# Moving one image's convolutions out of the head and running the last image's final stage in three lanes

## The chip, the cores and the metric

The kernel runs on one core of a Trainium2 chip. The metric is the device time of one execution in microseconds; the median of the runs is taken. A core has five engines that run their own instruction queues in order and wait for one another on semaphores: TensorE (PE, matmuls into PSUM), VectorE (DVE), ScalarE (ACT, activation functions from a loaded table set), GpSimd (POOL) and SyncE (SP), whose queue issues the kernel's DMAs.

## What is computed

Four layers follow one another on x of shape (4, 64, 64, 128), four images of 4096 pixels with 128 channels. The change touches layers 0 and 1 and the point at which layer 2 begins. Both are state-space scans in four directions over the pixels of an image:

```python
# layer 0, per image
left, right = jnp.split(x, 2, axis=-1)
right = _silu(_bn(_conv1x1(right, cv1_w), cv1_g, cv1_b))
xr = _ss2d(right, ...)            # in_proj, depthwise 3x3, Silu, four scans, norm, * silu(z), out_proj
l = _silu(_bn(_conv1x1(left, cv2_w), cv2_g, cv2_b))
l = _bn(l, bn0_g, bn0_b)
l = jax.nn.relu(_bn(_conv3x3(l, c1_w, c1_b), bn1_g, bn1_b))
l = jax.nn.relu(_bn(_conv3x3(l, c2_w, c2_b), bn2_g, bn2_b))
l = jax.nn.relu(_conv1x1(l, c3_w) + c3_b)
xr = _silu(_bn(_conv1x1(xr, cv_w), cv_g, cv_b))
out = _silu(_bn(_conv1x1(jnp.concatenate([l, xr], -1), cv3_w), cv3_g, cv3_b))   # shuffled, + x

# the scan of both layers, per direction
h = jnp.exp(d_t[..., None] * A) * h + (d_t * x_t)[..., None] * B_t[:, :, None, :]
y_t = jnp.einsum('bkdn,bkn->bkd', h, C_t)

# the end of layer 1, per image
y = _ln(y, onorm_w, onorm_b) * _silu(z)
x = input + y @ out_proj_w
h2 = _ln(x, ln2_w, ln2_b)
h2 = jax.nn.gelu(h2 @ fc1_w + fc1_b, approximate=False) @ fc2_w + fc2_b
return x + h2
```

Note that the 3x3 convolutions of layer 0 work on the left half of the channels. The scan of layer 0 doesn't read their result; it is joined to the scan's result afterwards.

## The kernel before

Everything is held channel by pixel: 128 partitions, an image's 4096 pixels along the free axis, worked on in eight chunks of 512 pixels (NCH = 8, T = 512) or, in the scans, in four steps of 1024 (TS).

The scans (class Scans, L240) are 3072 units: 12 tasks (one for each image in layer 0, two for each image in layer 1) of 4 directions, 4 steps and 16 groups. For each unit PE spreads the step sizes (L406), ACT takes the exponential in PSUM (L408), POOL forms the product dbu from a DMA'd tile dub and repB (L398), DVE scans (L418), copies a state (L428) and multiplies with repC (L430), and PE sums (L453). `run` issues this in a fixed order, u units ahead for each stage, and `prepare` makes the next step's operands.

Beside the scans runs the side work (class Side, L532): `pre0` (L786, before a layer 0 scan), `post0` (L844, after it), `pre1` (L888) and `post1` (L922) around the scans of layer 1. They are generators that yield the engine their next step needs. `order` (L988) lists them with the scan after which and before which each is due; PIECES (L984) gives the number of steps of each. After each unit `between` (L1034) hands out a credit of at least PACE = 0.83 steps, issues steps that `Lane.fits` lets through, and issues without asking when a due unit has come (`late`). Times in the planner (class Plan, L115) are estimates written by hand; it decides only the order in which instructions are issued. Stores of the side work are posted and issued later, on SP's queue.

Two pieces of side work stand outside the scans. `pre0(0)`, the head, runs before the first scan: per chunk a projection cv1 and cv2, Silu, the two halves of in_proj and a Silu of z; then `depthwise` (L676), eight half-image passes with a Silu each; then twice `conv` (L713), the 3x3 convolutions, and c3. Only after that does the first task fetch xc (L283) and prepare its first step. `post1(3)`, the tail, runs after the last scan, one chunk after the other: load y and silu(z), a norm over 256 channels (`norm`, L750), product, output projection, add, a norm over 128 channels, fc1 in four parts, Gelu, fc2, add, store. All side tiles and the side's PSUM bank `ms` have one buffer (`fetch` and `pad` two).

Every Silu and Gelu of the side work goes through `act` (L633), which puts the table set of Ln and Exp, the one the scans need, back at once:

```python
def act(self, out, in_, func, **kw):
    self.nc.scalar.activation(out, in_, func, **kw)
    self.nc.scalar.preload_act_table_set("natural_log_exp_and_others")
```

Side instructions go through a counting wrapper, so they all carry line L98 in the profile and are told apart by their tiles. After the tail the pools of the scans are given back and layer 2 (class Edges, L1073) takes the memory: it loads its weights (L1091 to L1097), folds constants, clears near and vals (L1171, L1174) and starts with statistics of image 0 (L1191 to L1210).

Of the kernel before, what the change touches and what calls it, by code (L numbers as in the profile page):

```python
# [9 lines left out]
F32 = mybir.dt.float32  # L10
# [7 lines left out]
P = 128  # L18
H = 64
HW = 64  # L20
L = HW * HW
T = 512
NCH = L // T
# [4 lines left out]
TS = 1024  # L28
# [86 lines left out]
class Plan:  # L115
# [16 lines left out]
    def start(self):  # L132
        self.at = dict(PE=0.0, ACT=0.0, POOL=0.0)
        self.done, self.running = 0.0, True
# [105 lines left out]
class Scans:  # L240
# [27 lines left out]
    def tile(self, name, bufs, tag=None, shape=(P, TS), dtype=F32):  # L268
        return self.pool.tile(list(shape), dtype, name=name, tag=tag or name, bufs=bufs)

    def bank(self):
        return self.psum.tile([P, T], F32, name="mp", tag="mp", bufs=1)
# [259 lines left out]
class Side:  # L532
# [100 lines left out]
    def act(self, out, in_, func, **kw):  # L633

        self.nc.scalar.activation(out, in_, func, **kw)
        self.nc.scalar.preload_act_table_set("natural_log_exp_and_others")

    def fetch(self, name, src):
        t = self.tile(name, bufs=2)
# [145 lines left out]

    def pre0(self, b):  # L786

        nc = self.nc
        wt = self.weights(self.d0a)
        cv12, inp, c3 = wt[:, 0:P], wt[0:H, P : 3 * P], wt[:, 3 * P : 3 * P + H]  # L790
        cw = wt[:, 3 * P + H :].rearrange("p (n t c) -> p n t c", n=2, t=6)
        lo, hi = slice(0, H), slice(H, P)
        x = self.fetch("x", self.x0[b, :, chunk(0)])
        for c in range(NCH):
            yield ("PE", self.landed) if c == 0 else "PE"
            ps = self.bank()
            nc.tensor.matmul(ps, cv12, x, start=True, stop=True)
            if c + 1 < NCH:
                x = self.fetch("x", self.x0[b, :, chunk(c + 1)])
            yield self.when("TAB", "d0")  # L800

            rl = self.tile("d0")
            self.act(rl, ps, AF.Silu, scale=self.cv12g, bias=self.cv12b)
            yield "PE POOL"
            l = self.tile("sq")
            nc.gpsimd.tensor_scalar(l[hi], rl[hi], self.bn0g[hi], self.bn0b[hi], ALU.mult, ALU.add)
            ps = self.bank()
            nc.tensor.matmul(ps, inp[:, 0:P], rl[lo], start=True, stop=True)
            yield self.when("ACT", "d1")
            xi = self.tile("d1")  # L810
            nc.scalar.copy(xi, ps)
            self.store("d1", self.xid[0, b, 0][:, chunk(c)], xi)
            self.store("sq", self.ld[b][0][:, chunk(c)], l[hi])
            yield "PE"
            ps = self.bank()
            nc.tensor.matmul(ps, inp[:, P : 2 * P], rl[lo], start=True, stop=True)
            yield self.when("TAB", "o")
            sz = self.tile("o")
            self.act(sz, ps, AF.Silu)
            self.store("o", self.szd[0, b, 0][:, chunk(c)], sz)  # L820
        yield from self.depthwise(self.dww0, self.dwb0, self.xid[0, b, 0], self.xcd[0, b, 0])
        for i in range(2):
            for item in self.conv(cw[:, i], self.ld[b][i]):
                if isinstance(item, str) or isinstance(item[0], str):
                    yield item
                    continue
                c, ps = item
                l = self.tile("d0")
                nc.scalar.activation(l, ps, AF.Relu, scale=self.bn12g[i], bias=self.cb[:, i : i + 1])
                if i == 0:  # L830
                    self.store("d0", self.across(self.ld[b][1], 0, H, c), l)
                    yield "PE"
                    continue
                yield "PE"
                ps = self.bank()
                for half in (lo, hi):
                    nc.tensor.matmul(ps[half, :], c3[half], l[half], start=True, stop=True)
                yield self.when("ACT", "o")
                o = self.tile("o")
                nc.scalar.activation(o, ps, AF.Relu, bias=self.c3b)  # L840
                self.store("o", self.across(self.catd[b], 0, H, c), o)
                yield "PE"
# [76 lines left out]
        for ct in range(2):  # L919
            yield from self.depthwise(self.dww1[:, ct, :], self.dwb1[:, ct, :], self.xid[1, b, ct], self.xcd[1, b, ct])  # L920

    def post1(self, b):  # L922
        nc = self.nc
        wt = self.weights(self.w1b)
        outp, fc1 = wt[:, 0:256].rearrange("p (t c) -> p t c", t=2), wt[:, 256:768]
        fc2 = wt[:, 768:1280].rearrange("p (t c) -> p t c", t=4)

        def start(c):
            big = self.tile("big", shape=(P, 4, T))
            for ct in range(2):  # L930
                nc.sync.dma_start(out=big[:, ct, :], in_=self.yd[1, b, ct][:, chunk(c)])
            for ct in range(2):
                nc.sync.dma_start(out=big[:, 2 + ct, :], in_=self.szd[1, b, ct][:, chunk(c)])
            self.landed = nc.now + FOUR_LANDING
            return [big[:, i, :] for i in range(2)], [big[:, i, :] for i in range(2, 4)]

        ys, szs = start(0)
        yield "PE", self.landed
        for c in range(NCH):
            ns = []  # L940
            yield from self.norm(ys, ns, "ACT")
            x = self.fetch("x", self.x1[b, :, chunk(c)])
            for ct, n in enumerate(ns):
                nc.scalar.activation(n, n, AF.Identity, scale=self.onw[:, ct : ct + 1], bias=self.onb[:, ct : ct + 1])
                yield "POOL"
                nc.gpsimd.tensor_mul(n, n, szs[ct])
                yield "ACT" if ct == 0 else "PE"
            ps = self.bank()
            for ct, n in enumerate(ns):
                nc.tensor.matmul(ps, outp[:, ct, :], n, start=ct == 0, stop=ct == 1)  # L950
            yield "ACT"
            x2 = self.tile("x2")
            nc.scalar.copy(x2, ps)
            yield "POOL"
            nc.gpsimd.tensor_add(x2, x2, x)
            yield "PE"
            ns = []
            yield from self.norm([x2], ns, "PE")
            (h2,) = ns
            hid = self.tile("hid", "big", (P, 4, T))  # L960
            for m in range(4):
                ps = self.bank()
                nc.tensor.matmul(ps, fc1[:, m * P : (m + 1) * P], h2, start=True, stop=True)
                yield "ACT"
                nc.scalar.activation(hid[:, m, :], ps, AF.Identity, bias=self.bias1[:, 4 + m : 5 + m])
                yield "PE" if m < 3 else "TAB"
            self.act(hid, hid, AF.Gelu)
            yield "PE"
            ps = self.bank()
            for m in range(4):  # L970
                nc.tensor.matmul(ps, fc2[:, m, :], hid[:, m, :], start=m == 0, stop=m == 3)
                yield "PE" if m < 3 else "ACT"
            o = self.tile("o")
            nc.scalar.activation(o, ps, AF.Identity, bias=self.fc2b)
            yield "POOL"
            nc.gpsimd.tensor_add(o, o, x2)
            if c + 1 < NCH:
                ys, szs = start(c + 1)
            yield "PE", self.landed
            self.store("o", self.x2[b, :, chunk(c)], o)  # L980

PIECES = dict(pre0=156, post0=114, pre1=172, post1=290)  # L984
PACE = 0.83


def order(nb):  # L988

    scans = [(layer, b) for layer in range(2) for b in range(nb)]
    side = []
    for b in range(1, nb):
        side.append(("pre0", b, None, (0, b)))
    side.insert(2, ("post0", 0, (0, 0), None))
    side.append(("pre1", 0, (0, 0), (1, 0)))
    for b in range(1, nb):
        side += [("post0", b, (0, b), None), ("pre1", b, (0, b), (1, b))]
    side += [("post1", b, (1, b), None) for b in range(nb - 1)]  # L1000
    at = {which: n for n, which in enumerate(scans)}
    side = [(name, b, at.get(after, -1), at.get(before, len(scans))) for name, b, after, before in side]
    return scans, side


def scan_layers(tc, C, nb, x_in, d0, s0, d1, s1, out):

    nc = tc.nc
    with ExitStack() as es:
        pool = es.enter_context(tc.tile_pool(name="scan", bufs=1))  # L1010
        side_pool = es.enter_context(tc.tile_pool(name="side", bufs=1))
        psum = es.enter_context(tc.tile_pool(name="psum", bufs=1, space=PSUM))
# [43 lines left out]
                credit -= 1.0  # L1056

        with tc.manual_schedule():
            for _ in side.pre0(0):
                pass  # L1060
            scans.run(between)
            plan.flush("side")
            plan.running = False
            for _ in side.post1(nb - 1):
                pass


NB = 9
# [766 lines left out]
```

## Time and profile before

| what | value |
|---|---|
| median of 3 runs | 14693.77 us (14692.58 to 14696.81) |
| the profiled execution | 14702.13 us, its span 14700.3 us |
| mean granted PE clock | 0.711 |
| first scan (L418) starts | 319.99 us |
| last scan starts | 11716.3 us |
| 3072 scans of DVE (L418), mean | 2.35 us with a state, 2.29 us without |
| hc products of DVE (L430), mean | 1.22 us |
| ACT_TABLE_LOAD of the side work, x640 | 821.1 us, 1.28 us each |
| first matmul of the tail | 11736.29 us |
| last add of the tail ends | 12154.6 us |

The profile is one execution. A row of the timeline gives start, duration, engine, line, operation, out<-in tiles, sizes and, in brackets, the idle time of the engine before it and what ended that. A row of the stages gives busy time and instruction count of each engine in that stretch, the share of full speed that the PE clock was granted, and the DMA engines' busy share and rate. L98 stands for all side work.

### The profile page before, as it was taken

Reading aid. Unit: us, or ns where it says so; the run is one execution under the profiler, and the core shown is the slowest. Engines: PE = TensorE matmul, PEld = TensorE weight load, DVE = VectorE, ACT = ScalarE, POOL = GpSimd, SP = SyncE. Lnnn points to the kernel's source line nnn. Section 1 sums busy time; section 2 is a strip of 40 time slices with the busy share of each in tenths; the row PEclk is TensorE's granted clock in tenths of the full one; section 3 lists DMA queues with packets and bytes.
Section 4 is the critical chain, followed back from the end, with each engine's and each line's share of the span. In section 5 each row is a group of like instructions: output and inputs, shape, how many; then the busy total and the mean of one; then the engine's idle time right before and its main releaser. Section 6 shows DMA issues by size and latency. Waiting matters only on the chain. (4 is left out here: it accounts for less than half of the span.)

```text
span 14700.3 us, 125581 instructions
## 1 busy us (share of the span) xinstructions
PE 10730.8 (73%) x36776; PEld 2755.0 (19%) x36776; DVE 12416.1 (84%) x10627; ACT 7877.7 (54%) x9279; POOL 9851.6 (67%) x4742
## 2 busy tenths in 40 slices
PE   5777777777776677777767767777776657777999
PEld 1111111111111111111111111111111112223555
DVE  1999999999999999999999999999999904565666
ACT  3645466555656565566555555555555335543555
POOL 1877788777888788788778888888888713441000
PEclk7676676766667666667667776667766568777999
DMA  4888888888888988988888777787787600002000
GB/s 113 220 207 218 204 216 222 216 214 217 216 224 215 224 208 208 230 217 211 216 213 213 199 195 200 197 208 200 196 205 193 166 30 24 20 18 48 13 14 8
DMA packets 853732, 2490.00 MB, mean 169 GB/s; under 512 B 143031, under 2 KB 164287, under 8 KB 844855
## 3 DMA queue, kind: packets, MB, share of 16 engines
q1 hardware_dynamic: 853047, 2481.97, 67.1%
q8 instruction: 295, 4.83, 0.1%
q14 instruction: 390, 3.19, 0.1%
HBM read 2060.21 MB, written 270.27 MB: 159 GB/s over the span
## 5 line engine op out<-in xcount | busy, mean ns | idle before, releaser
L398 POOL TENSOR_TENSOR dbu<-dub,repB 128x1024 f32<-128x1024 f32 x3072 | 7189.7, 2354 | 1511.2 <-DVE da L418 882.7
L418 DVE TENSOR_TENSOR_SCAN da<-da,state,dbu 128x1024 f32<-128x1024 f32 x2304 | 5415.4, 2350 | 297.3 <-ACT da L408 246.7
L408 ACT ACTIVATE da<-da,av 128x1024 f32<-128x1024 f32 x3072 | 3343.2, 1089 | 3647.8 <-PE da L406 3582.6
L406 PE MATMUL da<-dp,spread 96*128 96x512 bf16 x6144 | 2592.8, 516 | 2982.7 <-DVE hc L430 2959.1
L430 DVE TENSOR_TENSOR hc<-da,repC 128x1024 f32<-128x1024 f32 x3072 | 3741.0, 1218 | 40.5 <-PE ms L98 0.5
L453 PE MATMUL yps<-hc,gather 128*32 128x512 f32 x12288 | 2363.5, 852 | 2.3 <-DVE hc L430 2.3
L418 DVE TENSOR_TENSOR_SCAN da<-da,dbu 128x1024 f32<-128x1024 f32 x768 | 1759.2, 2291 | 400.7 <-POOL dbu L398 321.5
L406 PEld LDWEIGHTS <-spread 96*128 96x128 bf16 x6144 | 477.5, 107 | 6516.1 <-DVE hc L430 4124.8
L98 PE MATMUL ms<-d,wts 128*128 128x512 f32 (+3 forms) x960 | 782.0, 941 | 203.6 <-POOL d L98 140.7
L98 ACT ACT_TABLE_LOAD x640 | 821.1, 1283 | 126.8 <-DMA xcd<-o 90.8
L98 POOL TENSOR_TENSOR delta<-delta,low 128x1024 f32<-128x1024 f32 x192 | 452.3, 2356 | 529.9 <-ACT low L98 529.9
L98 PE MATMUL mp<-xd,dtw 8*128 8x512 f32 (+1 forms) x768 | 668.9, 965 | 28.7 <-DMA xd<-xdd 17.1
L98 ACT CAST parts<-delta 128x1024 bf16<-128x1024 f32 x384 | 400.5, 1043 | 295.8 <-POOL delta L98 278.3
L1371 POOL TENSOR_TENSOR acc<-acc,part 128x512 f32<-128x512 f32 x256 | 318.8, 1268 | 338.1 <-DVE part L1367 338.0
L446 PE MATMUL yps<-y,ident 128*128 128x512 f32 x576 | 520.3, 998 | 3.2 <-ACT y L471 3.2
L453 PEld LDWEIGHTS yps<-hc,gather 128*32 128x32 f32 x12288 | 283.9, 128 | 1190.3 <-issue 1184.5
L98 POOL TENSOR_TENSOR low<-delta,xc 128x1024 f32<-128x1024 f32 x192 | 501.1, 2610 | 1.7
L1615 ACT ACTIVATE s<-s,nmax 128x512 f32<-128x512 f32 x512 | 366.8, 718 | 248.7 <-DVE nmax L1612 243.9
L1282 ACT ACTIVATE hid<-hid,relb 128x1024 f32<-128x1024 f32 x288 | 320.3, 1145 | 323.0 <-DVE hid L1277 320.3
L98 ACT ACTIVATE low<-mp,av 128x512 f32<-128x512 f32 x384 | 264.1, 688 | 399.9 <-PE mp L98 397.7
L1277 DVE TENSOR_TENSOR hid<-cen,near 128x1024 f32<-128x1024 f32 x288 | 336.2, 1218 | 163.6 <-PE cen L1270 113.6
L98 PE MATMUL ms<-pad,diag 96*32 96x504 f32 (+1 forms) x2304 | 420.4, 824 | 64.0 <-ACT o L98 47.9
(230 smaller groups left out, 11780.3 us busy)
## 6 DMA issues: line engine op xcount, KB each, us to landing
dub<-dud SPq DMA_DIRECT2D x3072, 512.0 KB
dp<-parts SPq DMA_DIRECT2D x2304, 64.0 KB
repB<-xdd SPq DMA_DIRECT2D x192, 512.0 KB
repC<-xdd SPq DMA_DIRECT2D x192, 512.0 KB
dud<-low SPq DMA_DIRECT2D x192, 512.0 KB
pad<-xid SPq DMA_DIRECT2D x192, 256.0 KB
szd<-o SPq DMA_DIRECT2D x96, 256.0 KB
xcd<-o SPq DMA_DIRECT2D x96, 256.0 KB
```

The lines of the kernel that those rows point to most:

```text
L98: return call(*args, **kw)
L398: self.nc.gpsimd.tensor_mul(dbu, self.live.pop(("dub", u)), t.prepared[step]["B"])
L406: self.nc.tensor.matmul(da[:, cols], self.C.spread[:, jj, :], dp[:, j, cols], start=True, stop=True)
L408: self.nc.scalar.activation(da, da, AF.Exp, scale=t.W.a[:, at : at + 1])
L418: nc.vector.tensor_tensor_scan(da[:, way], da[:, way], dbu[:, way], 0.0 if step % NSTEP == 0 else t.states[step - 1][:, g : g + 1], ALU.mu ...
L430: nc.vector.tensor_mul(hc, da, t.prepared[step]["C"])
L446: self.nc.tensor.matmul(out, lhs, self.view(rhs, k, c, i, HALVES), start=True, stop=False)
L453: self.nc.tensor.matmul(self.live["yps"][32 * j : 32 * j + 32, cols], self.C.gather[:, jj, :], self.live["hc", v][:, cols], start=False, s ...
L1277: nc.vector.tensor_add(hid.rearrange("p i (r w) -> p (i r) w", w=HW), cen[pair].rearrange("p i (r w) -> p (i r) w", w=HW), self.near[m][s] ...
L1282: nc.scalar.activation(hid, hid, AF.Gelu, bias=self.relb[:, m, t : t + 1])
L1371: nc.gpsimd.tensor_add(acc, acc, part)
L1615: nc.scalar.activation(s[:, i, :], s[:, i, :], AF.Exp, bias=nmax[:, h : h + 1], accum_out=total[:, h : h + 1],)
```

## The change

Three edits are made together.

First, `pre0` is cut in two. `open0` loads 384 columns of the weights and does the projections and the depthwise part; `convs` loads the other 832 columns and does the 3x3 convolutions and c3. For images 1 to 3 `pre0` is still both in turn. For image 0 only `open0` runs ahead of the scans, and ("convs", 0) is put into the list of side work, behind pre0 of image 3 and ahead of post0 of image 0. Before, post0(0) stood ahead of pre0(3).

Second, `act` puts the set of Ln and Exp back only while the scans run (`nc.running`). In the head it is put back once, at the end. In the tail it isn't put back at all.

Third, post1(3) is made by three lanes that take chunks 0, 3, 6; 1, 4, 7; and 2, 5. The first lane is the old side with its tiles. The other two (class Aside) lay their tiles into the scans' xc0, xc1 and y, allotted once more, and take the scans' PSUM banks `mp` and `da`. The weights are loaded once. A loop issues one step of each lane in turn, so that the lanes' instructions alternate on every queue.

```diff
     def act(self, out, in_, func, **kw):
 
         self.nc.scalar.activation(out, in_, func, **kw)
-        self.nc.scalar.preload_act_table_set("natural_log_exp_and_others")
+        if self.nc.running:
+            self.nc.scalar.preload_act_table_set("natural_log_exp_and_others")
...
     def pre0(self, b):
 
+        yield from self.open0(b)
+        yield from self.convs(b)
+
+    def open0(self, b):
         nc = self.nc
-        wt = self.weights(self.d0a)
-        cv12, inp, c3 = wt[:, 0:P], wt[0:H, P : 3 * P], wt[:, 3 * P : 3 * P + H]
-        cw = wt[:, 3 * P + H :].rearrange("p (n t c) -> p n t c", n=2, t=6)
+        wt = self.weights(self.d0a[:, 0 : 3 * P])
+        cv12, inp = wt[:, 0:P], wt[0:H, P : 3 * P]
...
         yield from self.depthwise(self.dww0, self.dwb0, self.xid[0, b, 0], self.xcd[0, b, 0])
+
+    def convs(self, b):
+        nc = self.nc
+        yield "SP"
+        wt = self.weights(self.d0a[:, 3 * P :])
+        c3, cw = wt[:, 0:H], wt[:, H:].rearrange("p (n t c) -> p n t c", n=2, t=6)
+        lo, hi = slice(0, H), slice(H, P)
         for i in range(2):
             for item in self.conv(cw[:, i], self.ld[b][i]):
...
-    def post1(self, b):
+    def post1(self, b, chunks=range(NCH), wt=None):
         nc = self.nc
-        wt = self.weights(self.w1b)
+        wt = self.weights(self.w1b) if wt is None else wt
...
-        for c in range(NCH):
+        for c in chunks:
...
-            if c + 1 < NCH:
-                ys, szs = start(c + 1)
+            if c != chunks[-1]:
+                ys, szs = start(c + chunks.step)
...
+class Aside(Side):
+
+    def __init__(self, side, n, spans, bank):
+        self.__dict__.update(side.__dict__)
+        self.storing, self.free = set(), {}
+
+        parts = [span[:, i * T : (i + 1) * T] for span in spans for i in range(NCH)]
+        big, parts = n * NCH // 2, parts[NCH:]
+        self.big = spans[0][:, big * T : (big + 4) * T].rearrange("p (i t) -> p i t", i=4)
+        self.parts, self.turn, self.own_bank = dict(), 0, bank
+        names = ("d0", "d1", "sq", "x2", "o", "x", "x'")
+        for i, name in enumerate(names):
+            self.parts[name] = parts[n * len(names) + i]
...
-PIECES = dict(pre0=156, post0=114, pre1=172, post1=290)
+PIECES = dict(pre0=157, convs=66, post0=114, pre1=172, post1=290)
...
-    side.insert(2, ("post0", 0, (0, 0), None))
+    side[3:3] = [("convs", 0, None, None), ("post0", 0, (0, 0), None)]
...
-            for _ in side.pre0(0):
+            for _ in side.open0(0):
                 pass
+            nc.scalar.preload_act_table_set("natural_log_exp_and_others")
             scans.run(between)
             plan.flush("side")
             plan.running = False
-            for _ in side.post1(nb - 1):
-                pass
+            spans = [pool.tile([P, L], F32, name=name, tag=name, bufs=1) for name in ("xc0", "xc1", "y")]
+            wt = side.weights(side.w1b)
+            lanes = [side] + [
+                Aside(side, n, spans, bank)
+                for n, bank in enumerate((scans.bank, lambda: psum.tile([P, TS], F32, name="da", tag="da", bufs=2)[:, 0:T]))
+            ]
+            lanes = [lane.post1(nb - 1, range(n, NCH, 3), wt) for n, lane in enumerate(lanes)]
+            while lanes:
+                lanes = [lane for lane in lanes if next(lane, None) is not None]
```

More of the change, by code (lines that the diff above doesn't have):

```diff
@@ L935, in start @@
             return [big[:, i, :] for i in range(2)], [big[:, i, :] for i in range(2, 4)]
-        ys, szs = start(0)
+        ys, szs = start(chunks[0])
         yield "PE", self.landed
-        for c in range(NCH):
+        for c in chunks:
             ns = []
@@ L976, in post1, with tile, bank @@
             nc.gpsimd.tensor_add(o, o, x2)
-            if c + 1 < NCH:
-                ys, szs = start(c + 1)
+            if c != chunks[-1]:
+                ys, szs = start(c + chunks.step)
             yield "PE", self.landed
             self.store("o", self.x2[b, :, chunk(c)], o)
-PIECES = dict(pre0=156, post0=114, pre1=172, post1=290)
+class Aside(Side):
[9 more added lines that the diff above has]
+            self.parts[name] = parts[n * len(names) + i]
+    def tile(self, name, tag=None, shape=(P, T), bufs=1):
+        tag = tag or name
+        if tag == "big":
+            return self.big
+        if bufs == 2:
+            self.turn += 1
+            tag += "'" * (self.turn % 2)
+        return self.parts[tag]
+    def bank(self):
+        return self.own_bank()
+PIECES = dict(pre0=157, convs=66, post0=114, pre1=172, post1=290)
 PACE = 0.83
```

## The prediction

> **What bounds the kernel now.** I read the page first (busy shares, then the 40 slices), next busy time by stage, then the timeline of the two stages that the change touches.
>
> ```profile
> span 14700.3 us, 125581 instructions
> PE 10730.8 (73%) x36776; PEld 2755.0 (19%) x36776; DVE 12416.1 (84%) x10627; ACT 7877.7 (54%) x9279; POOL 9851.6 (67%) x4742
> DVE  1999999999999999999999999999999904565666
> ```
>
> VectorE is full from slice 2 to slice 32. The first slice and the two after slice 32 are a head and a tail in which it has nothing to do. By stage (columns as headed: busy time and instructions of each engine, granted clock, DMA share and rate):
>
> ```profile
> core 0: us, PE busy (x) PEld busy (x) DVE busy (x) ACT busy (x) POOL busy (x), PEclk, DMA share, GB/s
> 24.00:101.00 77.00, 49.70 (x48) 11.98 (x48) 0.00 (x0) 54.02 (x54) 7.24 (x11) 1.00 0.27 86
> 101.00:180.00 79.00, 40.67 (x192) 8.38 (x192) 0.00 (x0) 26.92 (x26) 1.16 (x8) 0.66 0.40 106
> 180.00:276.00 96.00, 54.74 (x208) 14.79 (x208) 0.00 (x0) 9.53 (x13) 0.29 (x2) 0.80 0.27 67
> 320.00:11720.00 11400.00, 8150.43 (x25160) 1700.58 (x25164) 10885.68 (x8460) 6351.78 (x6655) 9286.37 (x4266) 0.68 0.84 210
> 11725.00:12157.00 432.00, 240.75 (x303) 73.77 (x303) 18.27 (x53) 129.33 (x171) 77.61 (x60) 0.63 0.11 37
> ```
>
> Head (24 to 320 us): projections, depthwise, 3x3 convolutions, then loads and the first prepare. Nothing runs beside it, and the scans (320 to 11720) can't start sooner. Tail (11725 to 12157): image 3's post1, no engine over 56% busy, so latency bounds it. In both a shorter chain is a shorter kernel; in the scans only what stalls VectorE counts.
>
> Head timeline (start, duration, engine, line, what, idle before and releaser; the last lines jump):
>
> ```profile
> 141.17 1.28 ACT L98 ACT_TABLE_LOAD   x1 [6.17 <-DMA xcd<-o]
> 142.47 0.69 ACT L98 ACTIVATE o<-ms,v 128x512 f32<-128x512 f32 x1
> 143.17 1.28 ACT L98 ACT_TABLE_LOAD   x1
> ...
> 179.96 2.98 SPq L662 DMA_DIRECT2D pad<-ld  x4
> ...
> 276.17 1.89 SPq L283 DMA_DIRECT2D xc<-xcd  x4
> 284.71 1.98 PE L98 MATMUL mp<-xc,xp 128*64 128x512 f32 x4 [10.15 <-DMA xc<-xcd]
> 319.99 2.30 DVE L418 TENSOR_TENSOR_SCAN da<-da,dbu 128x1024 f32<-128x1024 f32 x1 [303.32 <-POOL dbu L398]
> ```
>
> Each Silu pays a load before it, after the awaited store has landed, and one after it under the next store. The convolutions fill 179.96 to 276.17. One chunk of the tail, at its Gelu and its end:
>
> ```profile
> 11778.46 1.28 ACT L98 ACT_TABLE_LOAD   x1
> 11779.75 1.91 ACT L98 ACTIVATE hid<-hid 128x2048 f32<-128x2048 f32 x1
> 11781.68 1.28 ACT L98 ACT_TABLE_LOAD   x1
> 11787.56 0.69 ACT L98 ACTIVATE o<-ms,v 128x512 f32<-128x512 f32 x1 [4.59 <-PE ms L98]
> ```
>
> **What the skill says.** (1) "ScalarE: Activation LUTs", What ACT_TABLE_LOAD costs: about 1.28 us a load plus a drain of 1.38. The trace has the 1.28, and back-to-back starts without that drain; I use 1.28. (2) The same page, Table sets: one set holds both Ln and Exp, but a load stands ahead of each activation that needs another set. In the trace of before, norm shows none between Ln and Exp, since `act` puts the joint set back each time. (3) "TensorE: Matmul & The Clock Gate", Part 1: the clock is halved until some 3.4 us of sustained work. The tail agrees: lone 128x512 matmuls take 2.07 us, those in a run about 1.0.
>
> **The change, part by part** (profiled execution: 14702.1 us; its span 14700.3).
>
> *Loads in the head.* The chunk loop's pitch is 9.79 us (Silu at 36.15, next 45.94); a load of 1.28 with its gaps, 1.33, stands between matmul and Silu. Seven go (the first set was loaded at 9.83): 9.3 us. The other loads there lie beside a matmul of 2.07 and give nothing. Depthwise: eight loads lie between the store's landing (or the matmul) and the Silu: 8 x 1.28 = 10.2. The eight after the Silu hide under stores of 7.4 us. The new single load at the end hides under the last store.
>
> *Convolutions out of the head.* 276.17 - 179.96 = 96.2. What is late next is the xc load: of its four pieces the third now waits for the last xcd store (5.9 us, 171.39 to 177.25), but the first matmul needs the first piece only. Before it came 8.5 us after issue, with all four sharing the engines; I take 5.8, so 2.7 more. Head: 9.3 + 10.2 + 98.9 = 118.4. If that matmul waits for the last store instead, 108; at best 120.
>
> *Convolutions beside the scans.* What 79 scans cost with an image's convolutions beside them, and without side work (columns: VectorE busy on L418, number of scans, clock, DMA):
>
> ```profile
> 839.00:1136.00 297.00, 182.22 (x79) 0.72 0.78 200
> 1599.00:1894.00 295.00, 181.86 (x78) 0.71 0.79 200
> 2723.00:3010.00 287.00, 182.31 (x79) 0.71 0.80 204
> 11434.00:11716.00 282.00, 184.28 (x79) 0.55 0.70 171
> ```
>
> 879/236 = 3.725 us a scan against 282/79 = 3.570: 0.155 x 79 = 12.2 us added. The side work has room: in the built program its last step moves from about scan 2980 to 3030 of 3072. Its DMAs count too: 4.2 MB of pad, 2.1 MB of stores and 0.4 MB of weights on SP's queue, ahead of the dub loads at times; the three windows contain the same for other images. Bounds: 1 (against the mean pitch 3.711) and 25 (double). pre1(0), due before scan 1001, ends near 995 instead of 940: tight, not late.
>
> *Tail.* Before: chunk pitch (12104.65 - 11790.67)/6 = 52.3; first matmul 11736.3 to last add 12154.6, 418.3 us. A chunk has 18 matmuls, 13.7 us of ScalarE without loads, 7 POOL products of 1.26. Three lanes step in turn, in order on every engine: 3, 3 and 2 chunks.
> Round 1, from its first matmul: 12 centring matmuls, 6.7 us cold and the rest warm, 15.6 (the other lanes' 2 MB arrive in 6 us at some 340 GB/s, within that); copy and six squares, then the last lane's sum 23.7, Ln and Exp 25.1. POOL has 12 products of 1.26 in order, ten of them after that: 37.8. Output projection, add, centring, square, sum, Ln and Exp of the last lane, 13.8: 51.6; product 52.9. Then ten of twelve fc1 matmuls with a cold start: 63.5; copy, one load, three Gelus: 71.2; fc2 runs from the first Gelu, 12 matmuls, 15.5: lane 1 ends at 81, and its next load takes 3.0 (as 11787.66 to 11790.67): 84.
> Round 2: `act` no longer puts the joint set back, and the built program has a load ahead of each Ln and each Exp: 12 in this round's two norms. A lane's pair grows from 1.35 to 3.88, three in a row 11.6. On the path that is 3.1 in the first norm (the sums come slower than the old pairs) and 7.6 in the second; 2 for a colder fc1: 97.
> Round 3, two lanes, the same steps: 75 to the last add.
> Sum 256 against 418.3: 162.3 won. Bounds: 90 if the matrix engine stays cold or lanes block one another, 195 if the products overlap better.
>
> *Layer 2's start.* Its setup (weights, memsets, near and vals on VectorE and POOL) ran beside the tail at 11733 to 11752. The lanes now hold xc0, xc1 and y, so in the built program it stands behind the tail: w is loaded after the last store lands (0.4 + 2.2), 0.5 MB about 3.5, sums 1.3, then the ping-pong of small matmuls (4.3, as 12153.24 to 12157.5), against 5.8 us from last add to first centring before. That is 6; gsp's Exp with a load stands ahead of the first copy, 2; a load between Ln and Exp of rstd, 1.3. POOL's four memsets, 7.7, fit in. Together 9 lost, bounds 4 and 14.
>
> **Sum.** -118.4 + 12.2 - 162.3 + 9 = -259.5: 14442.6 for the profiled execution. It lies 8.4 above the median of the three runs, 14693.8; so 14434.
>
> **Rivals.** *The lanes block one another.* Each lane has one PSUM bank, all queues are in order, 23 loads remain in the tail, and the clock may fall in each norm. For it: PE at 0.50 in most of the present tail. Against it: 12 fc1 and 12 fc2 matmuls in a row, enough to warm it. Gain 90 instead of 162: 14506. *Better overlap*, 195 in the tail and scans that pay nothing: 14389. *Crowded scans:* convolutions delay decay matmuls and dub loads (DMA share 0.84) and cost 60: 14482; the three windows speak against it. *Slower than before:* pre1(0) misses its date, and the planner then issues its steps by force in the scans' queues; every scan of layer 0 waits on its exponential. It decides from 259.5/3072 = 0.084 us per scan of the whole run, or 0.25 over layer 0's 1024, against 0.155 measured beside convolutions for 79. At 0.3 the time is 14741. *The change doesn't act:* the built program shows the loads gone and the order changed, so this is nearly nil.
>
> **Chances.** Forecast 0.66 (14400 to 14470), blocking lanes 0.12, better overlap 0.11, crowded scans 0.08, slower 0.02, no effect 0.01. For 8 in 10 the range reaches over half of the overlap case and of the crowded one: 14392 to 14486. Within 0.2% (29 us, what a measurement can tell from no change) 0.01, slower 0.02, faster 0.97.
>
> **What would show it.** Right: first scan near 201 us; mean pitch of scans up by 0.004; tail of three rounds near 84, 97 and 75 us with 23 loads; 16 us from the last add to layer 2's first centring copy. Wrong: rounds above 110; the pitch of layer 0's 1024 scans (320 to 4175 us, 3.765 each) up by more than 0.05; first scan later than 212.

## The result and the profile after

The changed kernel takes 14570.29 us (median of 4 runs, 14567.40 to 14573.89) against 14693.17 before (4 runs on the same chip): ratio 0.9917, 95% interval 0.9904 to 0.9929. It gains 123 us where 260 were forecast. Its profiled execution took 14573.12, with a span of 14571.1, so 129.2 us of span were won.

The page of the changed kernel, the lines that were shown of before:

```profile
span 14571.1 us, 125478 instructions
PE 10679.9 (73%) x36776; PEld 2744.3 (19%) x36776; DVE 12415.6 (85%) x10627; ACT 7822.9 (54%) x9243; POOL 9850.2 (68%) x4742
DVE  4999989899999999999999999999999925565666
```

The first slice is now almost half full and the hole behind the scans is smaller, as planned. But among the slices of the scans there are two 8s where before every one was a 9: VectorE has the same work (12415.6 us) and loses time inside the scans. The stages (columns as before; two pieces of the head, scans, tail):

```profile
core 0: us, PE busy (x) PEld busy (x) DVE busy (x) ACT busy (x) POOL busy (x), PEclk, DMA share, GB/s
24.00:93.00 69.00, 48.71 (x48) 11.49 (x46) 0.00 (x0) 15.67 (x24) 7.23 (x11) 1.00 0.32 101
93.00:164.00 71.00, 38.15 (x192) 8.72 (x192) 0.00 (x0) 6.78 (x9) 0.86 (x6) 0.69 0.46 123
203.00:11740.00 11537.00, 8218.14 (x25363) 1704.82 (x25364) 10883.25 (x8459) 6356.08 (x6667) 9286.12 (x4271) 0.68 0.83 208
11745.00:12003.00 258.00, 163.25 (x294) 60.71 (x289) 0.00 (x0) 137.08 (x176) 69.48 (x56) 0.78 0.17 59
```

VectorE is busy 10883 us in the scans, as before, but the scans take 11537 us instead of 11400. The tail's PE clock is 0.78 (0.63 before). The end of the head in the timeline:

```profile
159.38 1.28 ACT L1100 ACT_TABLE_LOAD   x1
159.99 7.61 SPq L283 DMA_DIRECT2D xc<-xcd  x4
168.08 1.97 PE L98 MATMUL mp<-xc,xp 128*64 128x512 f32 x4 [9.69 <-DMA xc<-xcd]
203.37 2.30 DVE L418 TENSOR_TENSOR_SCAN da<-da,dbu 128x1024 f32<-128x1024 f32 x1 [186.76 <-POOL dbu L398]
```

The single load of the head (L1100) ends before xc is even there. First scan: 203.37 us, 116.6 earlier.

What each part did, from the two profiled executions:

| part | forecast | measured |
|---|---|---|
| start to first scan (319.99 to 203.37) | -118.4 | -116.6 |
| first to last scan (11396.3 to 11536.1) | +12.2 | +139.9 |
| tail, first matmul to last add (418.3 to 242.2) | -162.3 | -176.1 |
| last add to layer 2's first centring copy (7.9 to 18.2) | +9 | +10.3 |
| all of layers 2 and 3 after that copy | 0 | +13.4 |

The scans are the miss. The other terms are near the forecast, except the last, to which the last section comes back. Where do the scans lose? PE's waits on transfers in the scans (us in total, times, longest) of the kernel before and of the changed one:

```profile
PE mp L98 <- DMA xc<-xcd: 25.9, 8, 8.3
PE ms L98 <- DMA x<-yd: 19.8, 4, 8.4
PE mp L98 <- DMA xd<-xdd: 17.1, 8, 7.9
PE ms L98 <- DMA pad<-ld: 14.4, 4, 6.1
```

```profile
PE mp L98 <- DMA xd<-xdd: 58.8, 12, 9.0
PE mp L98 <- DMA xc<-xcd: 55.1, 7, 18.3
PE ms L98 <- DMA pad<-ld: 31.8, 6, 11.0
PE ms L98 <- DMA x<-yd: 26.3, 4, 8.7
```

From the first scan to the last, all rows of this kind sum to 102 us before and to 205 after. Two thirds of the growth (71 of 103 us) are not on the convolutions' own tiles (pad<-ld) but on xc and xd, the operands with which the scans' own next step is prepared. A single scan's pitch shows the same: 53 pitches before were over 2 us longer than the undisturbed 3.53 us and lost 184 us; after it is 73, and 311 us. The many small delays stayed at 371 and 385. So the loss is some twenty long stalls more. The longest (17.8 us, at scan 492) in the timeline:

```profile
2079.33 10.03 SPq L372 DMA_DIRECT2D dp<-parts  x12
2083.78 2.35 DVE L418 TENSOR_TENSOR_SCAN da<-da,state,dbu 128x1024 f32<-128x1024 f32 x1
2089.45 0.58 SPq L617 DMA_DIRECT2D xcd<-o  x1
2090.08 1.02 SPq L283 DMA_DIRECT2D xc<-xcd  x2
2091.21 1.93 SPq L663 DMA_DIRECT2D pad<-xid  x3
...
2099.62 1.98 PE L98 MATMUL mp<-xc,xp 128*64 128x512 f32 x4 [18.28 <-DMA xc<-xcd]
...
2103.88 1.09 ACT L408 ACTIVATE da<-da,av 128x1024 f32<-128x1024 f32 x1 [20.40 <-PE da L406]
...
2105.07 2.36 DVE L418 TENSOR_TENSOR_SCAN da<-da,state,dbu 128x1024 f32<-128x1024 f32 x1 [17.61 <-ACT da L408]
```

It reads from the bottom up: the scan waits for its exponential, this for PE's da matmul, and PE stands in its queue at mp<-xc, the first projection of the next image. xc was put into SP's queue behind ten microseconds of dp<-parts and behind a depthwise store (xcd<-o), and is followed by pads (pad<-xid). It is scan 492, 20 before the next image begins at 512. Before, no depthwise pass ran there; with post0(0) behind pre0(3) one does. But the pass is not needed for the stall. In *convs_second* (experiment 2) none runs between scans 319 and 634, the convolutions' last matmul lies at scan 490, and scan 492 stalls for 14.8 us. First *convs_second*, then the kernel before, at the same place:

```profile
2077.54 11.35 SPq L372 DMA_DIRECT2D dp<-parts  x12
2088.93 1.08 SPq L283 DMA_DIRECT2D xc<-xcd  x2
2093.24 1.97 PE L98 MATMUL mp<-xc,xp 128*64 128x512 f32 x4 [14.55 <-DMA xc<-xcd]
```

```profile
2172.87 1.86 SPq L372 DMA_DIRECT2D dp<-parts  x3
2174.78 1.05 SPq L283 DMA_DIRECT2D xc<-xcd  x2
2178.88 1.98 PE L98 MATMUL mp<-xc,xp 128*64 128x512 f32 x4 [3.00 <-DMA xc<-xcd]
```

What goes with the long waits is the run of twelve dp<-parts (copies of a step's operands, which `prepare` means to spread over several scans) just ahead of xc. The fourteen kernels of this document that issue mp<-xc at once fetch 98 new images between their first and last scan. In 14 of these fetches the twelve copies stand in one run, and PE waits 11.1 to 20.8 us for xc; in the other 84 they are spread, and PE waits 9.4 us or less, but for two (12.9 and 16.4). The kernel before has no such run, the changed one two (scans 492 and 1004). That the copies come in a run because `prepare` came late in the plan is likely; no run here tests it.

### The profile page after: what moved, and what is told of

Same layout as the page of the kernel before. It is cut to its first block, busy times and chain, and to the rows that moved or that the text cites. A ratio compares the mean times of both kernels' runs of the same rounds, so it can differ in the third digit from the quotient of the medians.

```text
span 14571.1 us, 125478 instructions
## 1 busy us (share of the span) xinstructions
PE 10679.9 (73%) x36776; PEld 2744.3 (19%) x36776; DVE 12415.6 (85%) x10627; ACT 7822.9 (54%) x9243; POOL 9850.2 (68%) x4742
## 5 line engine op out<-in xcount | busy, mean ns | idle before, releaser
L98 PE MATMUL ms<-d,wts 128*128 128x512 f32 (+3 forms) x900 | 708.4, 915 | 160.4 <-POOL d L98 122.6
```

Source lines behind the costliest of these rows:

```text
L98: return call(*args, **kw)
```

## The experiments

Theory A: the loss belongs to where the side steps fall (order, alignment), not to the convolutions. Rivals: the convolutions' steps cost it themselves (C); the other edits do (B). Later came D (PE's queue stands behind operands that have not landed) and E (the move crowds the work that must be done before scan 1001).

All runs in one table. "Scans" is from first to last scan, "waits" the sum of PE's waits on DMAs between them, both of the profiled execution; the kernels before that ran beside them had medians of 14693 to 14708, the highest beside the four runs with the gate or PACE 0.95. Some differences are no more than scatter: *undo_move* and *undo_move_joint* have the same scans, as do *undo_late* and *undo_late_joint*, and their profiles differ by 2 and 9 us there; and layers 2 and 3 alone scatter by 21 us (last section). So a difference of under 10 us of scans, or 20 us of time, says little by itself.

| kernel | us | ratio to before (95%) | scans | waits |
|---|---|---|---|---|
| before | 14693 | | 11396 | 102 |
| changed | 14570.3 | 0.9917 (0.9904, 0.9929) | 11536 | 205 |
| undo_move | 14540.4 | 0.9896 (0.9881, 0.9911) | 11410 | 129 |
| order_only | 14592.7 | 0.9931 (0.9918, 0.9943) | 11467 | 170 |
| convs_second | 14544.9 | 0.9901 (0.9887, 0.9914) | 11518 | 185 |
| undo_move_joint | 14524.7 | 0.9885 (0.9872, 0.9899) | 11408 | 124 |
| order_gate | 14587.9 | 0.9914 (0.9897, 0.9931) | 11481 | 158 |
| gate | 14576.8 | 0.9912 (0.9897, 0.9927) | 11556 | 202 |
| pace95 | 14611.2 | 0.9933 (0.9918, 0.9948) | 11575 | 188 |
| gate95 | 14595.8 | 0.9925 (0.9910, 0.9939) | 11574 | 186 |
| xc_only | 14527.5 | 0.9886 (0.9870, 0.9903) | 11499 | 154 |
| late | 14514.2 | 0.9879 (0.9864, 0.9894) | 11482 | 72 |
| undo_late | 14508.6 | 0.9875 (0.9861, 0.9890) | 11384 | 56 |
| undo_pace86 | 14591.1 | 0.9929 (0.9914, 0.9944) | 11461 | 154 |
| defer | 14511.2 | 0.9871 (0.9854, 0.9887) | 11492 | 185 |
| defer_early | 14512.1 | 0.9874 (0.9859, 0.9888) | 11500 | 173 |
| undo_late_joint | 14504.6 | 0.9867 (0.9852, 0.9881) | 11393 | 53 |
| defer_early_late_joint | 14484.7 | 0.9853 (0.9839, 0.9868) | 11466 | 76 |
| repeat_convs | 14559.5 | 0.9907 (0.9890, 0.9923) | 11434 | 155 |
| defer_gate_late_joint | 14471.2 | 0.9844 (0.9829, 0.9859) | 11460 | 62 |

Below, "excess" of a stretch is its length less 3.6 us for each of its scans.

**1. The move undone; the order alone.** *undo_move*, edits to the changed kernel:

```diff
-            for _ in side.open0(0):
+            for _ in side.pre0(0):
-    side[3:3] = [("convs", 0, None, None), ("post0", 0, (0, 0), None)]
+    side.insert(2, ("post0", 0, (0, 0), None))
```

> The changed kernel with one part undone: image 0's convolutions are back in the head, and post0(0) is back at its old place in the list of side work. The split weight load, the single table load and the lanes of the tail stay. Theory A (the loss in the scans comes with the move of the convolutions, through stalls of in-order queues that meet late transfers): first scan near 301 us (320 less 19.5 of table loads), scans 11396 us from first to last as before (within 15), tail as in the changed kernel, so about 14693 - 19.5 - 165 = 14508, faster than the changed kernel's 14570. Rival B (the split weight load or the other edits cost the scans, not the move): scans stay near 11536, so about 14650.

First scan 301.9, scans 11410, 157 us won behind the scans: 14540, not 14508, but 30 us faster than the changed kernel. The move of the convolutions, taken alone, is a loss. B falls, apart from the 14 us by which these scans are longer than before, not much over the scatter: what differs there is the weights' second load and the shift it brings.

*order_only* is undo_move with `side.insert(3, ...)`.

> As the run with the move undone, but post0(0) stands behind pre0(3), as in the changed kernel's list: only the order of the side work differs, no work is added to the scans. If the new order is what costs (theory A, phase): scans 11396 plus 60 to 130, so 14570 to 14640. If the convolutions' own steps cost it (rival C: six weights' columns, pads and matmuls beside the scans): scans within 15 of 11396, so 14508 +- 15.

Scans 11467: 57 us for an order without added work (time: 52 us). The stretch of scans 484 to 520 alone grows from an excess of 3.9 to 21.4 us. What the convolutions add under the same order is then 11536 - 11467 = 69 us.

**2. Another place.** *convs_second*: `side[2:2] = [convs(0), post0(0)]`.

> The changed kernel with the same work beside the scans, but the pair convs(0), post0(0) one place earlier in the list, ahead of pre0(3). Theory A (phase): the long stalls fall elsewhere, and the sum of the stalls over 2 us in the scans (319 us in the changed kernel, 186 before) changes by 40 or more either way: 14450 to 14530 or 14610 and up. Rival C (the convolutions' own cost): scans within 20 us of the changed kernel's 11536, so 14570 +- 20.

14545, 25 us less than the changed kernel; but the stalls over 2 us sum to 313 us for 311, and the scans are 18 us shorter. A missed; C has the scans within its 20 us, and the time 5 us outside. The stalls did move, though. Here pre0(3) missed its date, scan 745: 46 convolution matmuls lie in the trace under scans 745 to 747, and the pitches of 747 and 748 are 10 and 17 us too long. So the forced issue that the prediction named for its slower case does occur, and it cost some 27 us here.

Set against *undo_move*, which has the same order, the convolutions cost 11518 - 11410 = 108 us of scans in this place, not 69. And the order that cost 57 us without them costs 18 with them (11536 - 11518). So neither has a price of its own; it depends on what else is in the plan.

**3. Depthwise steps kept away from a new image's fetch; a faster pace.** The gate, in `between` (set in `depthwise` and `convs`):

```diff
+                if not late and plan.rowing and 228 <= i < 250:
+                    break
```

> As the run that had only the order changed (14593), but no depthwise or convolution step is issued while the next task's xc is fetched (units 228 to 250 of each 256), unless its date has come; the steps follow right after. Theory A (a depthwise pass beside the fetch of a new image holds the queue through which xc comes): scans 484 to 520 fall from 21 us over a pitch of 3.6 back to 6 or less, and the stall of 12 us at scan 492 is gone: about 14570, 15 to 35 us less. If the place does not matter and the steps cost the same wherever they are: 14593 +- 8.

> The changed kernel with the same gate: no depthwise or convolution step in units 228 to 250 of each 256 unless due. Theory A: the 18 us stall at scan 492 goes (484 to 520 from 27 to 6 us); pre1(0), pushed back a little, still runs into its date at scan 1001, so 980 to 1016 stays at 25 us or more. About 14550. Rival C (the convolutions' steps cost what they cost, wherever they are): 14570 +- 8.

> The changed kernel with PACE 0.95 for 0.83: the side work is issued faster, so that pre1(0) is through before its date, scan 1001. If the forced steps there are what costs: 980 to 1016 falls from 29 to about 5 us over a pitch of 3.6, while a depthwise pass still meets the fetch at scan 492 (20 us or more in 484 to 520): about 14546. If a faster pace only crowds the scans: 14570 or more, layer 0 longer than 3933 us.

> The changed kernel with both the gate and PACE 0.95. If the two causes are separate and add: both stretches at 6 us or less, about 45 us less than the changed kernel, 14525, which would be the convolutions moved at a cost of some 90 us less the head's 99. If the scans' loss is the convolutions' own and only changes its place: 14570 +- 10.

The local effects came in part, and the scans got no shorter in any of the four. order_gate: excess of 484 to 520 from 21 to 12 (6 expected), and 520 to 608 from 25 to 38. gate: 27 to 16 there, but pre1(0) came to its date and 72 depthwise matmuls were issued under scan 1003; the two scans behind it started 24 and 18 us late. pace95: 980 to 1016 from 29 to 12, and 0 to 228 from 36 to 50, 1300 to 1900 from 89 to 127. gate95: 17 and 28 in the two stretches where 6 and 6 were expected, and 25 us more time than the changed kernel. Against the kernel before that ran beside it, order_gate is at 0.9914 and order_only at 0.9931, which would be the 15 to 35 us expected; the intervals overlap and the scans don't show it. A stall driven from one place comes back at another, so taking away one bad meeting doesn't win the loss back.

**4. PE's queue.** *xc_only*, in `prepare`; *late* adds LANDING 9 (6) and ROWS_LANDING 16 (12):

```diff
+            if step == 0 and self.plan.running:
+                yield "PE", self.plan.now + 10.0
             ps = self.bank()
```

> The changed kernel; the first projection of a new image's or tile's step (mp<-xc) is put into PE's queue 10 us after its xc load is issued, when it has likely landed, instead of at once. Theory D (PE's in-order queue stands behind an operand that has not landed; in the scans PE waits 205 us on DMAs in the changed kernel and 102 before): PE's wait on xc falls from 55 us to 15 or less, and the scans by as much, to about 11495; 14530. If those waits hide nothing that VectorE needs, or only turn into later ones: 14570 +- 12 with the wait on xc gone.

> As the run before, and the planner's estimates of a landing raised from 6 to 9 us and from 12 to 16 us for rows, so that the side's and the preparation's matmuls also enter PE's queue later. Theory D: PE's waits on DMAs in the scans fall from 205 us to below 110, scans to 11440 or less, about 14475. If the convolutions' work itself costs the time: waits fall, scans stay above 11515.

> The same later issue in the kernel with the convolutions back in the head (14540, scans 11410, PE's waits on DMAs 129 us). Theory D: waits fall to 70 or less, scans to 11350 to 11380, about 14490. If the plan of before is a lucky draw that any shift spoils: scans 11430 or more.

xc_only did what D said: PE's wait on xc from 55 us to 4, 51 us of waits gone in all, 37 us of scans, 43 us of time. late took 133 us of waits away but only 55 us of the scans, where D had asked for 95. The rest came back one queue further, at POOL, whose product waits for dub behind the side's loads on SP's queue. From its timeline (scan 372, 9.6 us):

```profile
1608.62 1.08 SPq L665 DMA_DIRECT2D pad<-ld  x2
1609.80 1.83 SPq L395 DMA_DIRECT2D dub<-dud  x3
1611.72 0.55 SPq L332 DMA_DIRECT2D repC<-xdd  x1
...
1625.08 2.34 POOL L400 TENSOR_TENSOR dbu<-dub,repB 128x1024 f32<-128x1024 f32 x1 [16.96 <-DMA dub<-dud]
...
1627.45 2.36 DVE L420 TENSOR_TENSOR_SCAN da<-da,state,dbu 128x1024 f32<-128x1024 f32 x1 [9.49 <-POOL dbu L400]
```

Here PE isn't late (its pad matmul waited 3.2 us); POOL stood 16.96 us for dub, which SP had queued behind the pads.

So D holds for part of the loss. undo_late gains too (scans 11384, 26 us less), so not every shift spoils the plan of before; it missed its 11350 to 11380 and 14490. And late less undo_late is still 97 us of scans: with the waits gone the move costs as much as the head wins.

**5. How good was the plan of before?** *undo_pace86*: PACE 0.86 in undo_move, no work added.

> The kernel with the convolutions back in the head, PACE 0.86 for 0.83, which adds no work and only shifts the steps. If the plan of before is a well chosen draw (theory A in its weaker form: any other alignment costs tens of us): scans 11440 to 11490, 14570 to 14620. If it is typical: scans within 15 of 11410, 14540 +- 15.

Scans 11461, 51 us longer, and 51 us of time. The plan of before is better aligned than these. Of the three shifts without new work (the split load, the order, the pace) none was free: 14, 57 and 51 us, the first near the scatter.

**6. The date, and the step by itself.** *defer* takes image 3's convolutions out of pre0(3) and puts them ahead of post0(3), so that the work due before scan 1001 is 757 steps as in *undo_move*, not 823 (PIECES gets open0=91):

```diff
-    side[3:3] = [("convs", 0, None, None), ("post0", 0, (0, 0), None)]
+    side[2:] = [("open0", 3, None, (0, 3)), ("convs", 0, None, None), ("post0", 0, (0, 0), None)]
...
-        side += [("post0", b, (0, b), None), ("pre1", b, (0, b), (1, b))]
+        side += [("convs", 3, None, None)] * (b == 3) + [("post0", b, (0, b), None), ("pre1", b, (0, b), (1, b))]
```

> The changed kernel, but image 3's convolutions, which nothing needs before its own post0, stand just ahead of that post0 instead of within pre0(3): the steps due before scan 1001 are 757 as in the kernel before, not 823. Theory E (the move costs because it crowds the work that has a date): 980 to 1016 falls from 29 us over a pitch of 3.6 to 6 or less, layer 0 from 3933 to 3885 or less, scans to about 11480, 14515; the depthwise pass beside the fetch at scan 492 stays. Rival C (convolution steps cost 70 us wherever they stand): layer 0 falls, layer 1 rises by as much, scans 11520 or more, 14555 or more.

*defer_early* has convs(0) and post0(0) ahead of open0(3).

> As the run before, with the order of the kernel before: convs(0) and post0(0) ahead of image 3's open0. Theory E: as the run before within 25 us either way, since convolution steps, not depthwise ones, now meet the fetch at scan 492; no stall at 1001. Rival C: scans 11520 or more.

defer: 14511, 59 us less; scans 44 us less (11 of the rest lie in layers 2 and 3), 39 of them in layer 0 (3933 to 3894), where the excess of 980 to 1016 falls from 28.7 to 6.2. That is E's stall gone, with layer 0 and the scans 9 and 12 us short of what E asked for; C's 11520 didn't come. Only 22 of the 44 us stand in that stretch, and to move 66 steps is also a shift, so the 44 are not shown to be the date's alone. In the changed kernel no burst of forced steps is seen there: its last depthwise matmul of pre1(0) lies at scan 998. But post0(1) then begins with its loads just where layer 1's first xc is fetched, behind twelve dp<-parts that take 16.11 us to issue (PE waits 14.95 us for xc at 4060.84). The other order gives the same within 8 us; there convolution steps meet the fetch at scan 492, again behind twelve dp<-parts in a run, and it stalls for 10.6 us.

*repeat_convs* is undo_move with convs(0) once more between post1(0) and post1(1), where nothing is due:

```diff
+    side.insert(len(side) - 2, ("convs", 0, None, None))
```

> The kernel with the convolutions in the head, with the whole of convs(0) once more beside the scans of layer 1, between post1(0) and post1(1) (near scan 2275 to 2360), writing the same values again: the step by itself, far from dates and from depthwise passes. If the prediction's price of the step is right and the loss is in the company it keeps: scans 2240 to 3071 grow by 10 to 25 us over the kernel without the repeat, and the time from 14540 to about 14555. If convolution steps cost it wherever they stand (rival C): 60 to 80 us more, 14600 to 14620.

The same 140 scans (2240 to 2380) in undo_move and here:

```profile
8669.41:9183.40 513.99, 362.67 (x1050) 82.40 (x1048) 495.70 (x390) 273.20 (x293) 438.03 (x201) 0.70 0.79 201
```

```profile
8679.52:9207.58 528.06, 389.14 (x1182) 75.34 (x1180) 496.93 (x390) 246.64 (x260) 421.67 (x191) 0.69 0.81 202
```

14.1 us more, and 14.5 us from there to the last scan; 19 us of time. (The scans ahead of it, where the plan only shifts, are 10 us longer.) In this place the step by itself costs what the prediction said (12.2, bounds 1 to 25). C, one high price wherever the steps stand, falls; the step by itself among the scans of layer 0 wasn't tried.

**7. The tail's table loads, and the best.** *undo_move_joint* sets a flag before the scans and lets `act` put the joint set back in the tail too: 16 loads there for 23.

```diff
-        if self.nc.running:
+        if self.joint:
...
+            side.joint = True
             scans.run(between)
```

> As the run with the move undone, with the joint table set of Ln and Exp put back after each Gelu of the tail as well (the head keeps its single load). Ten loads fewer in the tail and layer 2's first statistics. If the loads of rounds 2 and 3 lie on the path as the prediction has them (3.1 + 7.6 in round 2, the like for two lanes in round 3, 3.3 at the start of layer 2): 12 to 20 us less than the run with the move undone, about 14492. If they lie beside other work: within 4 us of it.

From the first matmul to the last add 230.3 us for 241.1, 10.8 less, and 16 us of time. The rounds took 82, 82 and 66 us, for 74, 94 and 73 in undo_move: the preload costs 8 us in round 1 and wins 11 and 7 in the others. "ScalarE: Activation LUTs" (section Table sets) of the Trainium skill says that one set holds both Ln and Exp, and with the preload this tail agrees: 16 loads, none between an Ln and its Exp. Without it the joint set isn't the one that gets loaded: round 2 has twelve loads for its six pairs.

> The convolutions in the head, mp<-xc 10 us after its load, landings planned at 9 and 16 us, and the joint set put back in the tail: 14508.6 less 16, about 14493. It is the partner of the run before: their difference is what the move is worth once the waits are gone. Theory E: 50 to 65 us; rival C: within 15 us.

> As defer_early, with mp<-xc 10 us after its load, landings planned at 9 and 16 us, and the joint table set put back in the tail. Theory E and D together: first scan 203, scans 11400 to 11430, joint tail 16 us less: about 14430. Rival C: scans 11470 or more, so 14495 or more, no better than the kernel with the convolutions in the head.

> Image 3's convolutions put off, no depthwise or convolution step in units 228 to 250 of each 256 unless due, mp<-xc 10 us after its load, landings planned at 9 and 16 us, the joint set put back in the tail. If the stalls at the fetches of new images are what is left (484 to 520 at 22 us): scans 11440, about 14455. If a stall removed at one place turns up at another, as the two gated runs before showed: scans 11465 or more, 14480 or more.

undo_late_joint missed its 14493 by 12 us, which is within the scatter (scans and layers 2 and 3 are 9 and 11 us longer than in undo_late). defer_early_late_joint missed E's 14430 by 55 us; its scans, 11466, are 36 us over E's bound and close to C's 11470, though the step by itself is cheap. The pair differs by 20 us of time, between E's 50 and C's 15: the move, with image 3's convolutions put off, pays, but little. The last kernel, between its two expectations, is the best of all, 14471 us: 99 us below the changed kernel and 222 below before, with the stretches 484 to 520 at 7.7 us and 980 to 1016 at 3.4. 520 to 608 rose to 35 in return (26 in defer). Its scans, 11460, are still 63 us above before's.

## Why the prediction was wrong

Head and tail came close to the forecast; the scans did not, and they took half of the gain. The forecast's own sign of that came: the pitch of layer 0's scans rose by 0.076 us (3.765 to 3.841), where 0.05 was the limit.

*Head.* Right. Loads: the chunk's pitch fell from 9.79 to 8.51 us, 1.28 for 1.33. The first matmul came 8.1 us after the xc load was issued, not 5.8; that is the missing 2 us.

*Tail.* Right in kind, 14 us too careful, and in part by luck. The rounds took 74, 95 and 73 us for 84, 97 and 75. Of the 10 us of round 1, five are POOL's: its first twelve products began at 17.7 us, with lane 1's root, and ran almost without a gap to 33.0, where I had ten of them wait for the last root (25.1) and end at 37.8. The second norm and fc1 took 2 us less each. Round 2 should have gained the same, and came only 2 us below its figure because its loads cost more than I had: it is 21 us longer than round 1, where 13 were forecast, and with the joint set put back the two rounds are equal (82 and 82).

*Layer 2's start.* 10.3 for 9. Layers 2 and 3 behind it do the same work in 13 us more, at a lower granted clock (last section). That I had at nothing. It happens to cancel with the tail's surplus: from the last scan to the end 152.4 us were won, 153.3 forecast.

*Scans: the step that failed.* "0.155 x 79 = 12.2 us added." The price of the step by itself was right: it measures 14 where it was tried. Wrong was to take it for the whole, 139.9 us in place of 12.2: the three windows it was read from lie between two images' fetches, and the sum let every other step stay where it was. The 140 us are, by pairs of runs: 14 for the shift by the split load (undo_move to before), 57 for post0(0) moved behind pre0(3) (order_only to undo_move), 14 for the convolutions' steps (repeat_convs), 44 that went when image 3's convolutions were put off (changed to defer). That is 129; 11 are left. These are differences of single pairs along one path and need not add: along the other (convs_second) the convolutions cost 108 us and the order 18. On either path most of the loss is in what the other steps newly meet. The prediction called pre1(0) "tight, not late". No burst of forced steps is seen, yet relieving it won up to 44 us.

*Rivals.* "Crowded scans" had the mechanism that the timelines show, transfers late and da matmuls held, at 60 us and a chance of 0.08. The time came near neither case. I took the three windows as proof against it, though they could only speak for their own surroundings. The forced steps of the slower rival cost about 25 us where they occurred (gate, convs_second), far from turning the sign. Its 14741 adds 0.3 us a scan without taking out the 12.2 already in the forecast; it should read 14729, which changes nothing.

*Open.* Why defer's scans are still 82 us above undo_move's, with 14 for the steps and 33 of the 82 in layer 1, isn't settled by a run. It is of the size that a bare shift costs here (51, 57). Which alignment is good can't be read from a mean; no run separates the cost of each meeting, nor shows why the dp<-parts come in a run.

## What to carry over

When side work is moved into a full pipeline, price not only its own steps but everything behind them in its queue: list what each moved step will newly meet, above all a new tile's fetch and a due date, and look at what stands ahead of that fetch on the queue that issues it. Read a step's price from windows that hold such meetings too, and put the bare effect of a shift, measured by shifting without adding work, into the range. Issue a consumer into an in-order queue only when its operand has likely landed; for one projection that was worth 43 us here (xc_only).

## What was not expected of the hardware

Layers 2 and 3, with the same instructions, took 13 us more in the changed kernel. Its two bulk stretches there (first line of each: layer 2's edge sums), before and after:

```profile
12235.00:13235.00 1000.00, 796.81 (x2202) 221.24 (x2202) 616.00 (x638) 525.78 (x574) 393.40 (x323) 0.76 0.06 19
13235.00:14700.00 1465.00, 1331.11 (x8542) 701.98 (x8538) 890.36 (x1451) 731.53 (x1726) 54.57 (x44) 0.90 0.08 21
```

```profile
12093.00:13099.00 1006.00, 803.38 (x2202) 223.56 (x2202) 615.73 (x638) 525.63 (x574) 393.43 (x323) 0.75 0.06 19
13099.00:14571.00 1472.00, 1337.75 (x8545) 709.11 (x8538) 890.20 (x1451) 730.31 (x1726) 54.56 (x44) 0.89 0.08 21
```

PE's busy time is 13 us longer for the same matmuls, at a granted clock 0.01 lower; the other engines' is the same. The tail ahead of them is denser, but that alone doesn't make them slow. From layer 2's first centring copy to the end, the twenty kernels of this document run the same instructions. They took 2530.3 us (undo_late) to 2551.3 (the changed kernel, the longest of all) with one profile each, and the mean granted clock of the stretch goes from 0.846 down to 0.835 with it. The kernel before stands at 2537.9, and four kernels with the three-lane tail are quicker than it (undo_late, order_gate, gate95, gate). So 21 us of such a difference can come with the clock that is granted there. What sets it is open.
